# Column halves for layer 1's attention products, and a moved multiply by C in layer 1's state-space mixer

## The chip, the core and the metric

The kernel runs on one core of one Trainium2 chip, as one launch. Its metric is the device time of that launch in microseconds. A core has a matrix engine (TensorE, PE in the views; its weight loads are PEld), a vector engine (VectorE, DVE), an engine for activation functions and copies (ScalarE, ACT), a general one (GpSimd, POOL) and a queue that issues transfers (SyncE, SP). TensorE multiplies a stationary operand ("weights", at most 128 rows by 128 columns) with streamed columns and writes to PSUM[...]. A product that needs fewer rows or columns can use a part of the array, a tile of it, and several tiles work at once.

## What is computed

A perceiver of four layers: a latent x of 2 x 256 tokens with 256 features attends to a context of 2 x 4096 tokens, then passes self-attention or a mixer, and a feed-forward part, in each layer. All of it is float32. Two parts of layer 1 matter here. The first is its cross-attention with 16 heads of 64 (written out from the kernel's names and the weights' shapes in the reference):

```python
B, S, D = (4, 512, 256)
H, DK, DV = (16, 64, 64)
'Wq': jax.random.normal(ks[3], (H, D, DK), jnp.float32) * sd, 'bq': ...
'Wo': jax.random.normal(ks[9], (H * DV, D), jnp.float32) * sd, 'bo': ...
```

For each head, queries come from the normalised latent, keys and values from the context, and x + softmax(q k^T) v Wo + bo goes on. The second is the state-space mixer:

```python
delta = jax.nn.softplus(dtr @ W_dt + 2.0 * dt_bias).reshape(b, l, G, D_STATE)
A = -jnp.exp(A_log).reshape(G, D_STATE, D_STATE)
a = jnp.exp(delta[..., None] * A)
bb = (delta * x)[..., None] * Bg[:, :, :, None, :]
...
_, h = lax.associative_scan(comb, (a, bb), axis=1)
y = jnp.einsum('blgpn,blgn->blgp', h, Cg).reshape(b, l, D_INNER)
y = (y + D * xf) * jax.nn.silu(z)
return y @ W_out
```

so h[t] = a[t] h[t-1] + bb[t] along the tokens, weighed by C and summed over the 16 states.

## The kernel before

The layers run one after the other. Every float32 product is two passes of TensorE, so one `matmul` of the code is two weight loads and two matmuls in the trace. In both parts below the order of the instructions on TensorE, VectorE, ScalarE and GpSimd is the order of the code (`in_order`, L338, ties each instruction to the one before on its engine).

**Layer-1 cross-attention (`l1_xattn`, L973).** A unit u is one pair of heads of one batch element: 8 pairs times 2 elements, 16 units. Each passes over the context in 8 blocks of 512 tokens; g counts all 128 blocks. A trip of the loop (L1158) does, on TensorE: `weigh` of block g-10 (L1090; probabilities times values, the two heads in the two halves of the array's columns, so its weights are 64 columns wide, 128 x 64); in some trips the products below; `keys` of block g+1 (L1019; 128 x 128 weights, 512 streamed columns, two of them, through the helper `mm`, L355); `values` of block g-9 (L1026; 128 x 128 weights, 128 streamed columns, 4 x 2 of them); `scores` of block g (L1037; the two heads in the two halves of the array's rows, 64 x 128 weights). Once in a unit come: `sums` at the end of the unit's last `weigh` (L1104; a product with ones, 64 columns wide), `out` at g % 8 = 2 (L1141), `query` at g % 8 = 5 (L1013), and at g % 8 = 0 `turned` (L1116, four transposes of the running maxima, between keys and values) and `repeat` (L1127, four more, between values and scores).

The other engines follow: ScalarE copies the scores to SBUF (L1058), VectorE keeps their maxima (L1061), later subtracts the unit's maximum (L1072), ScalarE takes the exponential (L1075), GpSimd adds up the totals (L1086). VectorE copies the values (L335), ScalarE the keys (L1024). `combine` (L1111) and `maxima` (L1122) are VectorE's, on either side of `turned`. PSUM has four banks "mm" (scores, query, sums, turned, out), two "tr" (keys, values), one "dec" (the repeated maxima) and one accumulator for `weigh`.

**Layer-1 mixer (`l1_attn`, L1224).** 64 columns of states are taken in 32 pairs. For pair k: `b_columns` (L1329) repeats B on TensorE and copies it on ScalarE; `drives` (L1336) makes the decay on ScalarE into a bank "dec" (L1343) and multiplies B by delta x on GpSimd (L1345); one step of the softplus of later columns goes to ScalarE and GpSimd (L1218, L1219) in each trip; `states` (L1351) repeats C on TensorE (L1326) into a bank "mm", and on VectorE scans the two batch elements one after the other (L1357) and multiplies by C (L1360); `add_up` (L1363) adds the states on TensorE (L1368). A trip issues states(k), b_columns(k+2), drives(k+1), add_up(k-1). There are three banks "mm", two "tr", two "dec".

Of the kernel before, what the change touches and what calls it, by code (L numbers as in the profile page):

```python
# [22 lines left out]
P = 128  # L23
B = 2
L = 256
# [4 lines left out]
KC = D // P  # L30
# [238 lines left out]
class Perceiver:  # L269
# [85 lines left out]
    def mm(self, out, pairs):  # L355

        for i, (lhsT, rhs) in enumerate(pairs):
            self.nc.tensor.matmul(out, lhsT, rhs, start=i == 0, stop=i == len(pairs) - 1)  # L358
# [614 lines left out]
    def l1_xattn(self, x, cpool):  # L973
# [9 lines left out]
        nc = self.nc  # L983
        with ExitStack() as s:
# [3 lines left out]
            xnT = self.to_T(self.layernorm(x))  # L988
            wq, wk, wv, wo = (self.weight(f"l1x_w{n}") for n in "qkvo")
# [8 lines left out]
            halves = [slice(0, 64), slice(64, 128)]  # L998
            order = [(hh, i) for i in range(2) for hh in range(2)]
            ctx, q, kT, v, score = {}, {}, {}, {}, {}  # L1000
            most, low, spread, total, av, sums, rec, z = {}, {}, {}, {}, {}, {}, {}, {}
# [7 lines left out]
            def for_values(g):  # L1009

                return ("k", g + 8) if g + 8 < G and (g + 8) // 64 == g // 64 else ("v", g)

            def query(u):  # L1013
                ps = self.bank([P, L])
                self.mm(ps, [(wq[:, k, ts(u % 8, P)], xnT[:, k, ts(u // 8, L)]) for k in range(KC)])
                q[u] = p2.tile([P, L], F32, name="qT", tag="qT")
                return lambda: nc.vector.tensor_scalar_add(q[u], ps, self.col("l1x_bq", u % 8))

            def keys(g):  # L1019
                pr = g // 8 % 8  # L1020
                ps = self.bank([P, 512], "tr")
                self.mm(ps, [(wk[:, k, ts(pr, P)], ctx["k", g][:, k, :]) for k in range(KC)])
                kT[g] = p2.tile([P, 512], F32, name="kT", tag="kT")
                nc.scalar.activation(kT[g], ps, AF.Identity, bias=self.col("l1x_bk", pr))  # L1024

            def values(g):  # L1026
                pr = g // 8 % 8
                ps = self.bank([P, 4, P], "tr")
                for i in range(4):
                    self.mm(  # L1030
                        ps[:, i, :],
                        [(ctx[for_values(g)][:, k, ts(i, P)], wv[:, k, ts(pr, P)]) for k in range(KC)],
                    )
                v[g] = p2.tile([P, 4, P], F32, name="v", tag="v", bufs=3)
                self.copy(g < G - 8, v[g], ps)
# [80 lines left out]
            def turned(u):  # L1116
                ps = self.bank([P, 4, P])
                for i in range(4):
                    nc.tensor.transpose(ps[:, i, :], low[u][:, i // 2, ts(i % 2, P)], self.ident)
                low[u] = ps  # L1120

            def maxima(u):  # L1122
# [18 lines left out]
            def out(u):  # L1141
                ps = self.bank([P, 2, D])
                for qt in range(2):
                    self.mm(ps[:, qt, :], [(z[u][:, ts(qt, P)], wo[:, u % 8, :])])
                two = y[:, ts(u // 8, 2), :]
                return lambda: nc.vector.tensor_add(two, ps, two)

# [9 lines left out]
            with self.in_order(e.PE, e.DVE, e.Activation, e.Pool):  # L1157
                for g in range(-1, G + 12):  # L1158
# [7 lines left out]
                    u = g // 8 - 1 if g % 8 == 0 and 0 < g <= G else None  # L1166
# [6 lines left out]
                    if g % 8 == 2 and made(g - 11):  # L1173
                        evacs.append(out((g - 11) // 8))
                    if (g == -1 or g % 8 == 5) and made(g + 3):
                        evacs.append(query((g + 3) // 8))
# [5 lines left out]
                    if made(g + 1):  # L1182
                        keys(g + 1)
                    if u is not None:
                        turned(u)
# [6 lines left out]
                    if made(g - 9) and g <= G:  # L1192
                        values(g - 9)
                    if made(g - 8) and g >= G:
                        values(g - 8)
# [28 lines left out]
    def l1_attn(self, x):  # L1224
# [3 lines left out]
        nc = self.nc  # L1228
        T = NT * P
        with ExitStack() as s:  # L1230
# [17 lines left out]
            xnT = self.to_T(self.layernorm(x))  # L1248
# [19 lines left out]
            low, high = pool.tile([P, 4, T], F32, name="low"), pool.tile([P, 4, T], F32, name="high")  # L1268
# [50 lines left out]
            pairs = [(j, q, rs) for j in range(4) for q in range(4) for rs in ((0, 1), (2, 3))]  # L1319
            spread, decay, drive, weighed, sums = {}, {}, {}, {}, {}  # L1320

            def columns(mat, rows_of, j, q, rs, tag):
                got = [self.bank([P, T], tag) for _ in rs]
                for r, ps in zip(rs, got):
                    rows = ts(r, 32)
                    nc.tensor.matmul(ps, mat[rows, ts(q, P)], rows_of[rows, j, :], start=True, stop=True)  # L1326
                return got
# [23 lines left out]
            def states(k):  # L1351
                got = columns(mats["c"], cT, *pairs[k], "mm")
                weighed[k] = []
                for a, bb, c in zip(decay.pop(k), drive.pop(k), got):
                    h = p4.tile([P, T], F32, name="state", tag="state")
                    for b in range(B):
                        nc.vector.tensor_tensor_scan(  # L1357
                            h[:, ts(b, L)], a[:, ts(b, L)], bb[:, ts(b, L)], 0.0, ALU.mult, ALU.add
                        )
                    nc.vector.tensor_mul(h, c, h)  # L1360
                    weighed[k].append(h)

            def add_up(k):  # L1363
                j, q, rs = pairs[k]
# [13 lines left out]
            with self.in_order(e.PE, e.DVE, e.Activation, e.Pool):  # L1378
                n = len(pairs)
                for k in range(-2, n + 1):  # L1380
                    if 0 <= k < n:
                        states(k)
                    if k + 2 < n:
                        b_columns(k + 2)
                    if 0 <= k + 1 < n:
                        drives(k + 1)
                    step = next(made, None)
                    if step is not None:
                        step()
                    if k > 0:  # L1390
                        add_up(k - 1)
                self.conv_hidden("tr", "tr", "dec")
                return self.linear(yz, wout, x)
# [1196 lines left out]
```

## Time and profile before

Three runs took 2627.75, 2615.05 and 2627.32 us, median 2627.32. The execution that was profiled took 2616.86 us, of which the span from the first instruction to the last is 2615.1.

| | whole span | attention, 310 to 1240 us |
|---|---|---|
| length, us | 2615.1 | 930.0 |
| TensorE busy, us | 2480.0 (95%) | 928.83 |
| its weight loads, us | 1659.1 (63%) | 643.38 |
| VectorE busy, us | 1713.5 (66%) | 695.14 |
| ScalarE busy, us | 1343.4 (51%) | 582.28 |
| GpSimd busy, us | 919.3 (35%) | 546.43 |
| granted TensorE clock | 0.96 | 1.00 |

The largest groups of matmuls in the attention, by line, operands, weights' shape, streamed columns and count, with busy time and mean length of one:

```profile
L1051 PE MATMUL ps_mm<-qT,kT 64*128 64x256 f32 x2048 | 255.7, 389 | 0.0
L1098 PE MATMUL acc<-S,v 128*64 128x256 f32 x2048 | 250.1, 385 | 0.5 <-DVE rec L1136 0.4
L358 PE MATMUL ps_tr<-ctxT,w_l1x_wk 128*128 128x512 f32 x512 | 250.6, 612 | 0.0
L358 PE MATMUL ps_tr<-w_l1x_wv,ctxT 128*128 128x128 f32 x2048 | 249.9, 275 | 0.0
```

A row of such a view names the line, the engine, what is written from what, and the shape: "128*64" is rows by columns of the weights, "128x256" the streamed operand. A matmul's length includes its way through the array, so lengths overlap; the distance between starts is what a matmul costs. The keys and values carry the helper's line, L358.

### The profile page before, as it was taken

To read this page: it belongs to the slowest core of one execution; us is meant where nothing else is said; L and a number is where in the kernel's file an instruction comes from. 1 tells how busy PE (TensorE), PEld (TensorE's weight loads), DVE (VectorE), ACT (ScalarE), POOL (GpSimd) and SP (SyncE) were. 2 spreads that over 40 slices of the span, in tenths; PEclk is the share of its full clock that TensorE was granted. 3 is DMA by queue.
4 is the path that set the end of the run, shared out by engine and by line. 5 is a ranking of instruction groups with operands and counts; after the bars stand their busy time and mean duration, and the time that the engine had idled before them with its cause. 6 is when DMAs were issued, how large, how long until landed. Compare 5 with 4: busy or idle time off the path is not lost.

```text
span 2615.1 us, 45590 instructions
## 1 busy us (share of the span) xinstructions
PE 2480.0 (95%) x17701; PEld 1659.1 (63%) x17701; DVE 1713.5 (66%) x3184; ACT 1343.4 (51%) x2540; POOL 919.3 (35%) x864
## 2 busy tenths in 40 slices
PE   8987999999999999999799998899989999999889
PEld 6854566666666666666533565556935666664678
DVE  5566577777777777777769755544267888854642
ACT  3323666666666666666466421432215777784512
POOL 0520255555555555556639413001101222210010
PEclk9988999999999999999899998789999999999889
DMA  6210322222232222222210100005730000003656
GB/s 256 89 57 30 118 65 65 67 72 65 65 113 82 70 69 65 65 67 81 80 65 1 65 20 22 4 25 214 266 147 18 2 2 2 2 2 123 218 213 223
DMA packets 77255, 214.24 MB, mean 82 GB/s; under 512 B 6408, under 2 KB 21456, under 8 KB 66544
## 3 DMA queue, kind: packets, MB, share of 16 engines
q1 hardware_dynamic: 72128, 202.69, 23.4%
q0 software_dynamic: 1888, 5.90, 0.7%
q8 instruction: 139, 2.28, 0.4%
q10 hardware_dynamic: 3024, 2.75, 0.3%
q14 instruction: 76, 0.62, 0.1%
HBM read 190.48 MB, written 20.84 MB: 81 GB/s over the span
## 4 chain that ended last, share of the span: by engine, by line
PE 39%; DVE 6%; issue 2%; ACT 2%; POOL 2%; DMA 0%; another core or an unknown queue 0%; DVEq 0%; ACTq 0%; POOLq 0%; SPq 0%
PE ps_mm L358 10%; PE ps_mm L2172 5%; PE ps_tr L2216 5%; PE ps_tr L2200 4%; PE ps_tr L358 3%; PE acc L358 3%; PE ps_mm L785 2%; DVE state L1357 1%; POOL spread L1345 1%; PE ps_tr L2335 1%; PE acc L826 1%; PE ps_tr L801 1%; PE ps_tr L2378 1%; PE ps_mm L2360 1%; PE acc L1583 1%
## 5 line engine op out<-in xcount | busy, mean ns | idle before, releaser
L1086 POOL TENSOR_TENSOR total<-total,S 128x512 f32<-128x512 f32 x434 | 540.8, 1278 | 299.6 <-ACT S L1075 299.2
L1075 ACT ACTIVATE S<-S 128x512 f32<-128x512 f32 x512 | 302.3, 625 | 209.0 <-DVE S L1072 208.8
L2176 DVE TENSOR_REDUCE mx<-ps_mm 128x1 f32<-128x512 f32 x512 | 317.9, 684 | 73.0 <-PE ps_tr L2200 54.2
L1061 DVE TENSOR_TENSOR most<-ps_mm,most 128x512 f32<-128x512 f32 x448 | 278.3, 684 | 119.2 <-ACT S L1058 119.2
L1058 ACT COPY S<-ps_mm 128x512 f32<-128x512 f32 x512 | 262.8, 600 | 115.3 <-PE ps_mm L1051 114.5
L1072 DVE TENSOR_TENSOR S<-S,ps_dec 128x512 f32<-128x512 f32 x512 | 317.6, 680 | 1.3 <-PE ps_dec L1130 1.3
L2204 ACT ACTIVATE PT<-ps_tr 128x512 f32<-128x512 f32 x476 | 246.7, 603 | 74.6 <-PE ps_tr L2200 71.8
L358 PEld LDWEIGHTS ps_tr<-w_l1x_wv,ctxT 128*128 128x128 f32 x2048 | 246.9, 192 | 52.5 <-issue 52.2
L1051 PE MATMUL ps_mm<-qT,kT 64*128 64x256 f32 x2048 | 255.7, 389 | 0.0
L1098 PE MATMUL acc<-S,v 128*64 128x256 f32 x2048 | 250.1, 385 | 0.5 <-DVE rec L1136 0.4
L358 PE MATMUL ps_tr<-ctxT,w_l1x_wk 128*128 128x512 f32 x512 | 250.6, 612 | 0.0
L2172 PE MATMUL ps_mm<-kT,qT 32*128 32x512 f32 x1024 | 250.1, 618 | 0.2 <-DVE mx L2176 0.2
L358 PE MATMUL ps_tr<-w_l1x_wv,ctxT 128*128 128x128 f32 x2048 | 249.9, 275 | 0.0
L2200 PE MATMUL ps_tr<-qm,kT 32*128 32x256 f32 x1904 | 238.3, 388 | 0.0
L1051 PEld LDWEIGHTS ps_mm<-qT,kT 64*128 64x128 f32 x2048 | 187.3, 186 | 38.3 <-DVE most L1061 3.8
L1098 PEld LDWEIGHTS acc<-S,v 128*64 128x64 f32 x2048 | 136.1, 136 | 97.3 <-ACT S L1058 38.8
L2200 PEld LDWEIGHTS ps_tr<-qm,kT 32*128 32x128 f32 x1904 | 171.0, 184 | 15.6 <-issue 6.2
L2225 POOL TENSOR_TENSOR sums<-sums,part 128x256 f32<-128x256 f32 x102 | 73.7, 722 | 257.1 <-ACT part L2224 257.1
L358 PEld LDWEIGHTS ps_tr<-ctxT,w_l1x_wk 128*128 128x128 f32 x512 | 89.2, 189 | 100.6 <-issue 99.1
L335 DVE COPY v<-ps_tr 128x512 f32<-128x512 f32 x120 | 82.9, 690 | 89.0 <-PE ps_tr L358 88.9
L2216 PE MATMUL ps_tr<-PT,v 128*32 128x256 f32 x2048 | 139.6, 385 | 0.3 <-ACT PT L2204 0.3
L2172 PEld LDWEIGHTS ps_mm<-kT,qT 32*128 32x128 f32 x1024 | 86.3, 185 | 61.3 <-issue 49.9
(542 smaller groups left out, 3808.8 us busy)
## 6 DMA issues: line engine op xcount, KB each, us to landing
ctxT<-in_ctxT SPq DMA_DIRECT2D x144, 512.0 KB, 3.6
ctxT<-in_ctxT SPq DMA_DIRECT2D x16, 1024.0 KB, 5.7
w_l2f_gu<-in_l2f_gu SPq DMA_DIRECT2D x16, 1024.0 KB, 7.1
bd_dram<-bd SPq DMA_DIRECT2D x8, 1536.0 KB, 5.5
w_l3f_w<-in_l3f_w SPq DMA_DIRECT2D x11, 1028.0 KB, 9.8
w_l3f_w<-in_l3f_w SPq DMA_DIRECT2D x11, 1024.0 KB, 5.1
ctx<-in_ctx SPq DMA_DIRECT2D x8, 1024.0 KB, 4.9
w_l2f_down<-in_l2f_down SPq DMA_DIRECT2D x16, 512.0 KB, 5.3
```

The source lines that it names most:

```text
L358: self.nc.tensor.matmul(out, lhsT, rhs, start=i == 0, stop=i == len(pairs) - 1)
L1051: nc.tensor.matmul(banks[hh, i][:, j, :], k[part, ts(2 * i + j, P)], q[u][part, :], start=True, stop=True)
L1058: nc.scalar.copy(t, ps)
L1061: nc.vector.tensor_tensor(m, ps, m, ALU.max)
L1072: nc.vector.tensor_tensor(t, t, spread[u][:, hh, :].unsqueeze(1).to_broadcast([P, 2, L]), ALU.add)
L1075: nc.scalar.activation(t, t, AF.Exp)
L1086: nc.gpsimd.tensor_add(tot, tot, t)
L1098: nc.tensor.matmul(av[u][part], vs[:, 2 * i + j, part], got[hh, i][:, j, :], start=g % 8 == 0 and i + j == 0, stop=g % 8 == 7 and i + j == 2,)
L2172: nc.tensor.matmul(ps, qT[rows, 2 * half + c, ts(t, P)], kT[rows, ts(j, 512)], start=True, stop=True,)
L2176: nc.vector.tensor_reduce(mx[:, c, r, j : j + 1], ps, AX.X, ALU.max)
L2200: nc.tensor.matmul(ps[:, i, :], kT[rows, ts(2 * u + i, P)], q[rows], start=True, stop=True)
L2216: nc.tensor.matmul(ps[ts(r, 32), :], v[:, 2 * u + i, :], pt[:, i, :], start=i == 0, stop=i == 1)
```

## The change

In the attention a local `mm` replaces the helper for query, keys, values and out, and the transposes of `turned` become products with the identity through it too. It issues every product twice, for weight columns 0 to 63 and 64 to 127, the second half into the other 64 partitions of the same bank. `scores`, `weigh`, the sums and `repeat` stay as they were. In the mixer the multiply by C of a pair's first column is issued after the first scan of its second column; before, it came ahead of it. Nothing is moved past a transfer, and the order on ScalarE, GpSimd and SyncE is the same.

```diff
+            def mm(ps, pairs):
+
+                for k, (a, b) in enumerate(pairs):
+                    for part in halves:
+                        nc.tensor.matmul(ps[part], a[:, part], b, start=k == 0, stop=k == len(pairs) - 1)
+
             def query(u):
                 ps = self.bank([P, L])
-                self.mm(ps, [(wq[:, k, ts(u % 8, P)], xnT[:, k, ts(u // 8, L)]) for k in range(KC)])
+                mm(ps, [(wq[:, k, ts(u % 8, P)], xnT[:, k, ts(u // 8, L)]) for k in range(KC)])
...
-                self.mm(ps, [(wk[:, k, ts(pr, P)], ctx["k", g][:, k, :]) for k in range(KC)])
+                mm(ps, [(wk[:, k, ts(pr, P)], ctx["k", g][:, k, :]) for k in range(KC)])
...
                 for i in range(4):
-                    self.mm(
+                    mm(
                         ps[:, i, :],
                         [(ctx[for_values(g)][:, k, ts(i, P)], wv[:, k, ts(pr, P)]) for k in range(KC)],
                     )
...
                 for i in range(4):
-                    nc.tensor.transpose(ps[:, i, :], low[u][:, i // 2, ts(i % 2, P)], self.ident)
+                    mm(ps[:, i, :], [(low[u][:, i // 2, ts(i % 2, P)], self.ident)])
...
                 for qt in range(2):
-                    self.mm(ps[:, qt, :], [(z[u][:, ts(qt, P)], wo[:, u % 8, :])])
+                    mm(ps[:, qt, :], [(z[u][:, ts(qt, P)], wo[:, u % 8, :])])
...
-                for a, bb, c in zip(decay.pop(k), drive.pop(k), got):
+
+                for i, (a, bb) in enumerate(zip(decay.pop(k), drive.pop(k))):
                     h = p4.tile([P, T], F32, name="state", tag="state")
+                    weighed[k].append(h)
                     for b in range(B):
                         nc.vector.tensor_tensor_scan(
                             h[:, ts(b, L)], a[:, ts(b, L)], bb[:, ts(b, L)], 0.0, ALU.mult, ALU.add
                         )
-                    nc.vector.tensor_mul(h, c, h)
-                    weighed[k].append(h)
+                        if (i, b) == (1, 0):
+                            nc.vector.tensor_mul(weighed[k][0], got[0], weighed[k][0])
+                nc.vector.tensor_mul(h, got[1], h)
```

## The prediction

> **What bounds the kernel now.** I read the busy table by stretches first, then TensorE's timeline within the layer-1 attention, then VectorE's, TensorE's and GpSimd's timelines within the mixer. Columns of the first view: stretch, then for each engine busy us (instructions), granted clock, DMA share, GB/s.
>
> ```profile
> 400.00:500.00 100.00, 99.83 (x699) 69.52 (x698) 73.62 (x118) 62.42 (x115) 57.88 (x47) 1.00 0.22 65
> 600.00:700.00 100.00, 99.83 (x697) 69.62 (x698) 73.82 (x118) 62.37 (x115) 58.78 (x48) 1.00 0.23 66
> ...
> 1362.00:1382.00 20.00, 20.00 (x64) 7.28 (x63) 18.96 (x32) 14.82 (x27) 16.48 (x14) 1.00 0.00 2
> ```
>
> In attention TensorE alone is full at full clock; VectorE (74%), ScalarE (62%), GpSimd (58%) and the DMA have room. In the mixer TensorE is full too and VectorE at 95%.
>
> Busy does not mean streaming, so I took the starts (start us, length, engine, line, operation, count):
>
> ```profile
> 746.93 1.95 PE L1098 MATMUL acc<-S,v 128*64 128x256 f32 x16
> 748.71 1.08 PE L358 MATMUL ps_mm<-total,ones 128*64 128x256 f32 x8
> 749.72 1.98 PE L358 MATMUL ps_tr<-ctxT,w_l1x_wk 128*128 128x512 f32 x4
> ...
> 763.71 1.95 PE L1098 MATMUL acc<-S,v 128*64 128x256 f32 x16
> 765.59 1.98 PE L358 MATMUL ps_tr<-ctxT,w_l1x_wk 128*128 128x512 f32 x4
> 767.41 1.95 PE L358 MATMUL ps_tr<-w_l1x_wv,ctxT 128*128 128x128 f32 x16
> 769.29 2.00 PE L1051 MATMUL ps_mm<-qT,kT 64*128 64x256 f32 x16
> ...
> 780.60 1.13 PE L358 MATMUL ps_mm<-xT,w_l1x_wq 128*128 128x256 f32 x4
> 781.56 1.88 PE L358 MATMUL ps_tr<-ctxT,w_l1x_wk 128*128 128x512 f32 x4
> 783.28 1.95 PE L358 MATMUL ps_tr<-w_l1x_wv,ctxT 128*128 128x128 f32 x16
> ```
>
> Start to start, weigh (L1098, 64 weight columns) takes 748.71-746.93 = 1.78 us when 64-column work follows, but 765.59-763.71 = 1.88 us when full-width keys follow. Keys take 767.41-765.59 = 1.82 us right after weigh, but 783.28-781.56 = 1.72 us after the full-width query. So the step from 64-column to full-width tiles costs 0.10 + 0.10 = 0.20 us (93 + 104 = 197 ns by the trace's starts): TensorE empties, then the first load is not hidden. One context block is weigh 1.88 + keys 1.82 + values 1.88 + scores 1.93 = 7.51 us.
>
> Does a half-width product keep pace at 128 streamed columns, as values would? Layer 3 has it:
>
> ```profile
> 2438.75 1.08 PE L2390 MATMUL acc<-PT,values 128*32 128x128 f32 x32
> 2439.76 0.59 PE L2335 MATMUL ps_tr<-rT,qv 32*128 32x384 f32 x2
> ```
>
> 32 matmuls in four column tiles, 8 rounds, 1.01 us to the next tile shape; less 0.09 to empty and 0.05 for the first load, 0.109 us a round.
>
> In the mixer VectorE runs scan, scan, multiply by C (L1360), and again:
>
> ```profile
> 1452.73 1.26 DVE L1357 TENSOR_TENSOR_SCAN state<-ps_dec,spread 128x256 f32<-128x256 f32 x2
> 1454.10 0.69 DVE L1360 TENSOR_TENSOR state<-ps_mm,state 128x512 f32<-128x512 f32 x1
> 1454.71 1.26 DVE L1357 TENSOR_TENSOR_SCAN state<-ps_dec,spread 128x256 f32<-128x256 f32 x2
> ```
>
> A column takes 1454.71-1452.73 = 1.975 us, a pair 3.95. The starts are 0.60 (scan), 0.77 (scan to multiply), 0.61 (multiply to scan): the multiply waits 0.17 us for the scan it reads. TensorE's own pair, where it never stops, is
>
> ```profile
> 1365.90 1.98 PE L1368 MATMUL acc<-state,ident 128*128 128x512 f32 x4
> 1367.81 1.13 PE L1326 MATMUL ps_mm<-cT,mat_c 32*128 32x512 f32 x4
> 1368.78 1.02 PE L1326 MATMUL ps_tr<-bT,mat_b 32*128 32x512 f32 x4
> 1369.73 1.98 PE L1368 MATMUL acc<-state,ident 128*128 128x512 f32 x4
> ```
>
> 3.83 us, and GpSimd's two spread products plus one delta product 2.50 + 1.27 = 3.77 us.
>
> **What the Trainium skill says.** "TensorEngine Tiling (Array Packing)", Key Properties: "Changing tiling mode (not just tile) drains the TensorE"; tiles load and multiply in parallel. The trace agrees: 0.197 us at weigh to keys, nothing at weigh to sums. Same page, Restrictions: column tiling excludes transpose mode for FP32; that is why `turned` becomes a plain matmul. "TensorE: Matmul & The Clock Gate", LDWEIGHTS: load time goes with weight columns; here loads read 137 ns at 64 columns, 190 at 128. "VectorE: DVE Perf Modes", The DRAIN you can't avoid: a same-engine read after write needs a semaphore or one intervening VectorE op; the 0.77 against 0.60 us above is that semaphore.
>
> **The change, part by part.** Sums are against the profiled execution: 2616.86 us, span 2615.1.
>
> *Weigh to keys.* Weigh, sums, out, query, keys, turned and values now all have 64-column tiles, so the change of shape after weigh goes: 0.197 us. Values to scores and scores to weigh keep theirs. Weigh meets keys in blocks g = 10 to 127, 118 times; 14 of them (g = 16, 24, ... 120) hold the turned maxima and are counted apart. 104 x 0.197 = 20.5 us.
>
> *Pace of keys and values.* Twice the matmuls at half the width, two at a time: keys stay at 0.429 us a round (weigh's pairs keep full pace: 0.216 us per 256 columns, 0.429/2). Values now need (1.88-0.09)/16 = 0.1115 us a round; I take the 0.109 of L2390: 16 x 0.0023 = 0.037 us, 104 times, 3.8 us. Bounds: 0 if the 0.1115 stays; a loss if rounds get longer (rival C).
>
> *Blocks with the turned maxima.* In the same timeline four transposes took 742.39-741.95 = 0.44 us; as fp32 matmuls each makes two passes, 8 rounds x 0.109 = 0.87: +0.44. After values the repeat (L1130, full width) now meets a change of shape. From weigh: 1.73 + 1.72 + 0.87 + 1.75 + 0.09 = 6.16 us to the repeat. Before, it began at 744.42, weigh at 738.25, 6.17 us earlier, because it waited for VectorE's reduction of the maxima, which ends when VectorE's queue allows. Thus 0, bounds -0.2 to +0.1 us each, -3 to +1.4 in all.
>
> *Start and end of attention.* Blocks 0 to 7 alternate keys and scores; the load after scores is 64 columns, 8 x 0.05 = +0.4 us, paid back by the first turned (+0.44), on which all engines wait. In the last blocks (g > 127) values and weigh alternate without any change of shape, 0.34 us for each of 6 blocks, but TensorE already waits 3.62 us for GpSimd's totals there: no gain. The last turned sits on the path: -0.5 us.
>
> What hides the rest: VectorE needs 0.74 x 7.51 = 5.6 us of a block of 7.27. The copied values land 1.1 us before weigh, the exponentials 1.6 us, the banks of scores 3 us: no wait takes over 0.23 us. Context loads are at 24% of the DMA. Sum: 20.5 + 3.8 + 0 - 0.5 = 23.8 us. What follows starts with the mixer's weight load (win, 6.84 us), which is issued when attention's buffers are freed, so it moves along.
>
> *Mixer.* New order: scan, scan, scan, multiply first column, scan, multiply second. The first multiply's input is finished during the third scan, so one of two 0.17 us waits goes: VectorE's pair 3.95 - 0.17 = 3.78 us. Then TensorE's 3.83 is late next, and GpSimd's 3.77 is close: 0.12 us for each of the some 26 pairs from 1362 us on: 3.1 us. Before 1362 TensorE is the bound (projections between): 0. The moved multiply passes only the third scan, which needs the second column's decay and spread; ScalarE can make that decay once the scans of the previous pair's second column are through, over 1 us ahead. It frees its C bank 0.43 us later; the bank is wanted some 2 us later. Bounds: 0 (GpSimd's chain with delta keeps 3.95) to 5 us (0.17 x 27 and the hiccups at each eighth pair shrink). I take 3.
>
> Sum: 23.8 + 3 = 26.8 us.
>
> **From sum to forecast.** The executions of before lie at two levels, 2615.05 and 2616.86, and 2627.32 and 2627.75; the profile doesn't say why. 26.8 off the profiled 2616.9 is 2590; off the median 2627.3 it is 2600.5. I forecast 2597, between, nearer the median.
>
> **Rivals.**
> *B: half of it.* A bank or semaphore wait hides behind the 0.09 us in which TensorE empties and stays, or the turned blocks lose their 0.2 us, or the mixer gives nothing. For: out and query take banks of scores, whose release the emptying would mask. Against: weigh to sums runs on without a gap. 10 to 14 us gained: 2613 to 2617 from the median.
> *C: slower.* The two halves of one product stream the same columns, and 4 instructions are due every 0.109 us; if halves run one after the other, or instructions come too late, values pay. It decides from 0.109 + 0.234/16 = 0.124 us a round; at 0.15 us 118 x (16 x 0.041 - 0.197) = 54 us are lost: 2680; fully serial, values and keys cost 1.7 us each a block, over 400 us. For: weigh's halves stream different data. Against: L2390 does 8 instructions in 0.109 us over a run of 64, as long as the 64 of values; the rest of a block is sparser.
> *D: the mixer turns against itself,* as the first accumulate or ACT waits: 2 to 3 us back, 2602; it stays within the forecast's range.
>
> **Chances.** Forecast, with D, 0.78 (its own range 2586 to 2606: 21 to 31 us off either level); B 0.16; C 0.06. About 0.5%, 13 us, is what a measurement of this kernel can tell from no change. B falls half on each side of it: faster 0.78 + 0.08 = 0.86, same 0.08, slower 0.06. The range reaches into B: 2584 to 2614.
>
> **What would show it.** Weigh to keys 1.73 us start to start and keys 1.72 in every block; a block 7.27 us; values 16 rounds in 1.84 to the scores; turned 0.87; TensorE's matmuls up by 2880 (512 keys, 2048 values, 64 query, 64 out, 192 turned); the mixer's pair 3.83 us with TensorE without gaps, VectorE's first multiply 0.60 us after the third scan. The prediction is wrong if rounds of values exceed 0.124 us, if keys still start 0.3 us after weigh's last matmul, or if the mixer's pair stays at 3.95.

## The result and the profile after

The changed kernel took 2594.41, 2588.19, 2587.97 and 2593.47 us, median 2590.83; the kernel before, beside it, 2627.75, 2615.05, 2627.32 and 2617.16, median 2622.24. The ratio is 0.9884, with a 95% interval of 0.986 to 0.9908: a gain of 24 to 37 us. The profiled execution took 2594.41 us with a span of 2592.6.

The busy table by stretches of the changed kernel (stretch, length; for PE, PEld, DVE, ACT and POOL busy us and instructions; granted clock, DMA share, GB/s):

```profile
400.00:500.00 100.00, 100.00 (x1000) 68.72 (x998) 77.39 (x123) 64.08 (x118) 57.96 (x48) 1.00 0.23 70
600.00:700.00 100.00, 100.00 (x986) 68.58 (x986) 76.80 (x122) 62.97 (x117) 58.29 (x47) 1.00 0.24 70
1362.00:1382.00 20.00, 20.00 (x66) 7.17 (x68) 19.22 (x32) 13.33 (x24) 19.90 (x17) 1.00 0.00 0
```

TensorE still is the full engine. That its share only rose from 99.83 to 100.00 while the stage became 24 us shorter shows how little this figure can tell. VectorE, with the same work in less time, went from 74 to 77%. The groups of matmuls in the attention (310 to 1215 us) show the new shapes:

```profile
L1017 PE MATMUL ps_tr<-w_l1x_wv,ctxT 128*64 128x128 f32 x3744 | 225.0, 273 | 0.0
L1017 PE MATMUL ps_tr<-ctxT,w_l1x_wk 128*64 128x512 f32 x936 | 221.4, 592 | 0.0
```

Keys and values are now "128*64" and carry the line of the local `mm`, L1017; a matmul of values is as long as before (273 against 275 ns), though there are twice as many of them. Now the order on TensorE (start us, length, engine, line, operation, count), first four blocks without extras, then one with the turned maxima:

```profile
753.26 1.89 PE L1017 MATMUL ps_tr<-ctxT,w_l1x_wk 128*64 128x512 f32 x8
754.98 1.92 PE L1017 MATMUL ps_tr<-w_l1x_wv,ctxT 128*64 128x128 f32 x32
756.82 2.00 PE L1057 MATMUL ps_mm<-qT,kT 64*128 64x256 f32 x16
758.75 1.95 PE L1104 MATMUL acc<-S,v 128*64 128x256 f32 x16
760.53 1.89 PE L1017 MATMUL ps_tr<-ctxT,w_l1x_wk 128*64 128x512 f32 x8
...
788.69 1.95 PE L1104 MATMUL acc<-S,v 128*64 128x256 f32 x16
790.47 1.89 PE L1017 MATMUL ps_tr<-ctxT,w_l1x_wk 128*64 128x512 f32 x8
792.18 1.04 PE L1017 MATMUL ps_mm<-ident,low 128*64 128x128 f32 x16
793.05 1.92 PE L1017 MATMUL ps_tr<-w_l1x_wv,ctxT 128*64 128x128 f32 x32
794.90 0.65 PE L1136 MATMUL ps_dec<-ident,nm 128*128 128x128 f32 x4
```

Read the distances of the starts: keys 754.98-753.26 = 1.72 us, values 1.84, scores 1.93, weigh 760.53-758.75 = 1.78. A block is 7.27 us where it was 7.50. The starts of `weigh`, one line for the eight blocks of a unit (the one with 8.7 holds the turned maxima; 8.1 to 8.4 hold out, query or sums), show that the gain is the same in every other block:

```
before  8.37 7.50 7.50 8.37 7.50 7.50 8.68 8.42
after   8.13 7.27 7.27 8.13 7.27 7.27 8.72 8.18
```

In the mixer, VectorE of the changed kernel:

```profile
1428.21 1.84 DVE L1365 TENSOR_TENSOR_SCAN state<-ps_dec,spread 128x256 f32<-128x256 f32 x3
1429.97 0.66 DVE L1369 TENSOR_TENSOR state<-ps_mm,state 128x512 f32<-128x512 f32 x1
1430.55 0.68 DVE L1365 TENSOR_TENSOR_SCAN state<-ps_dec,spread 128x256 f32<-128x256 f32 x1
1431.33 0.69 DVE L1370 TENSOR_TENSOR state<-ps_mm,state 128x512 f32<-128x512 f32 x1
1431.94 1.84 DVE L1365 TENSOR_TENSOR_SCAN state<-ps_dec,spread 128x256 f32<-128x256 f32 x3
```

VectorE's pair is 1431.94-1428.21 = 3.73 us (3.95 before): three scans 1.76, the first multiply 0.58 without a wait, the fourth scan 0.78 to the multiply that reads it, and 0.61. TensorE takes 3.83 without a gap (its sums of two neighbouring pairs start at 1428.90 and 1432.73). The distances between the starts of the sums of neighbouring pairs, from the third sum to the last, tell where the mixer's time went:

```
before  3.83 x11, 3.88 3.95 4.67 3.88 3.95 3.94 3.95 3.95 3.95 3.95 4.67 3.89 3.95 3.95 3.95 3.09 3.95 2.90
after   3.83 x15, 3.87, 3.83 x10, 2.97 3.30 2.68
```

For 11 distances the two kernels are alike; only then had VectorE of before fallen behind far enough for TensorE to wait for it. The trace of before shows this lead shrink by about 0.12 us a pair: the first multiply of a pair ends 3.73 us ahead of the sum at 1369.73, 2.02 us ahead of the one at 1404.2, and 1.96 us ahead of the one at 1408.1, where the distances start to grow.

Now the whole, cut at the starts of named instructions. "Blocks" is from the first `weigh` to the last `scores`, "tail" from there to the last `out`, "start" from the mixer's first product to its first sum, "pairs" from there to the first product of layer 2, "rest" from there to the end, and the last column is how long TensorE's clock stood at half in the rest (a stretch at half clock that the end of the kernel cuts off isn't counted).

| kernel | span | blocks | tail | start | pairs | rest | half clock in the rest |
|---|---|---|---|---|---|---|---|
| before | 2615.1 | 936.76 | 53.37 | 43.87 | 126.53 | 1137.45 | 150.18 |
| after | 2592.6 | 912.96 | 54.64 | 45.61 | 122.00 | 1140.82 | 160.43 |

Blocks -23.8, tail +1.3, pairs -4.5: 27.0 us in the stretches that the change touches. The spans differ by 22.5 only, because start and rest, in which both kernels issue the same products, were 5 us longer in this execution.

### The profile page after: what moved, and what is told of

Its sections match the earlier page's. It is cut to its first block, busy times and chain, and to the rows that moved or that the text cites. A ratio compares the mean times of both kernels' runs of the same rounds, so it can differ in the third digit from the quotient of the medians.

```text
span 2592.6 us, 51423 instructions
## 1 busy us (share of the span) xinstructions
PE 2457.8 (95%) x20579; PEld 1637.4 (63%) x20581; DVE 1709.5 (66%) x3184; ACT 1342.6 (52%) x2540; POOL 921.2 (36%) x864
## 4 chain that ended last, share of the span: by engine, by line
PE 41%; DVE 5%; issue 2%; ACT 2%; POOL 1%; DMA 0%; DVEq 0%; ACTq 0%; POOLq 0%; SPq 0%
PE ps_mm L358 10%; PE ps_mm L2181 5%; PE ps_tr L2225 5%; PE ps_tr L2209 4%; PE ps_tr L358 3%; PE acc L358 3%; PE ps_mm L785 2%; PE ps_tr L2344 1%; DVE state L1365 1%; PE acc L826 1%; PE ps_tr L2387 1%; POOL spread L1351 1%; PE ps_tr L801 1%; PE acc L1377 1%; PE acc L1592 1%
## 5 line engine op out<-in xcount | busy, mean ns | idle before, releaser
L1017 PEld LDWEIGHTS ps_tr<-w_l1x_wv,ctxT 128*64 128x64 f32 x4096 | 235.4, 137 | 58.4 <-issue 57.7
L1017 PE MATMUL ps_tr<-w_l1x_wv,ctxT 128*64 128x128 f32 x4096 | 248.2, 273 | 0.0
L1017 PE MATMUL ps_tr<-ctxT,w_l1x_wk 128*64 128x512 f32 x1024 | 242.4, 593 | 0.4 <-PE ps_mm L1017 0.4
L1017 PEld LDWEIGHTS ps_tr<-ctxT,w_l1x_wk 128*64 128x64 f32 x1024 | 75.8, 137 | 91.3 <-issue 74.7
```

Of the source, the lines that this page charges most:

```text
L1017: nc.tensor.matmul(ps[part], a[:, part], b, start=k == 0, stop=k == len(pairs) - 1)
```

## The experiments

Two questions were open: whether the attention's gain comes from the removed change of tile shape or from the half width itself (each product cheaper), and whether the mixer gives anything. Diffs are against the changed kernel.

| run | median us (of one run where no ratio stands) | ratio to before, interval | blocks | tail | start | pairs | rest | half clock |
|---|---|---|---|---|---|---|---|---|
| attn_only | 2598.63 | 0.9917 [0.9903, 0.9931] | 912.96 | 56.07 | 43.75 | 126.55 | 1135.11 | 143.36 |
| mixer_only | 2613.80 | 0.9967 [0.9955, 0.9979] | 936.78 | 53.94 | 46.21 | 122.05 | 1139.42 | 150.19 |
| mixer_third | 2609.97 | 0.9979 [0.9959, 0.9999] | 936.73 | 53.80 | 46.69 | 122.03 | 1128.08 | 136.53 |
| values_full | 2616.78 | 0.9977 [0.9966, 0.9987] | 938.67 | 53.81 | 43.87 | 122.01 | 1130.88 | 143.36 |
| turned_transposed | 2587.82 | 0.9867 [0.9850, 0.9884] | 912.31 | 54.74 | 46.75 | 121.99 | 1137.50 | 150.18 |
| halves_in_series | 2596.12 | 0.9890 [0.9871, 0.9909] | 918.34 | 55.00 | 46.84 | 122.00 | 1135.67 | 146.77 |
| no_wait_multiplies | 2593.35 | 0.9884 [0.9866, 0.9902] | 912.97 | 54.67 | 45.67 | 122.60 | 1137.64 | 153.60 |
| last_totals_on_pe | 2586.78 | 0.9863 [0.9843, 0.9882] | 912.97 | 50.16 | 43.72 | 122.32 | 1138.36 | 153.60 |
| sums_in_twos | 2605.17 | 0.9942 [0.9925, 0.9959] | 912.97 | 54.67 | 52.70 | 130.91 | 1137.52 | 150.19 |
| both_more | 2599.36 | 0.9922 [0.9901, 0.9943] | 912.96 | 50.16 | 53.17 | 127.57 | 1146.26 | 177.49 |
| before_again | 2617.54 | | 936.73 | 53.71 | 46.42 | 126.47 | 1134.99 | 143.36 |
| mixer_again | 2609.22 | | 936.72 | 53.27 | 43.63 | 121.98 | 1136.09 | 143.36 |

A stretch repeats within 0.1 us in "blocks", and within 0.4 in "pairs", where it isn't edited; "start" swings by 3 us and "rest" by 18 where nothing in them was changed. In `attn_only` the tail is 56.07 us, because the clock stood at half for a further 3.41 us in it, from 1226.80 us on. So the stretches carry the findings below, and the times check them.

**The two parts alone.** Attention alone:

```diff
-                for i, (a, bb) in enumerate(zip(decay.pop(k), drive.pop(k))):
+                for a, bb, c in zip(decay.pop(k), drive.pop(k), got):
...
-                        if (i, b) == (1, 0):
-                            nc.vector.tensor_mul(weighed[k][0], got[0], weighed[k][0])
-                nc.vector.tensor_mul(h, got[1], h)
+                    nc.vector.tensor_mul(h, c, h)
+                    weighed[k].append(h)
```

> Only the attention's column halves; the mixer as before. If the halves carry the gain: from the first weigh to the last scores 913 us as in the changed kernel (936.8 before), VectorE's pair in the mixer back at 3.95 us, from the mixer's first sum to its end 126.5 us; time 0.990 to 0.991 of before, some 25 us less. If the mixer carries more than its 3 us, or helps the attention, this one stays at 0.995 or above.

The mixer alone is the other half: the kernel before with the new `states`.

> Only the moved multiply; the attention as before. If one of two 0.17 us waits goes and TensorE is late next: from the mixer's first sum to its end 122 us (126.5 before), pairs at 3.83 us with TensorE without gaps, time 0.998 to 0.999 of before, which is below what this kernel's time can tell. If the 4.5 us seen in that stretch were chance of the clock or of the start, it stays at 126 us.

The blocks gain all their 23.8 us with attention alone and nothing with the mixer alone; the pairs the other way round, 4.5. The parts don't touch each other. In time, attention alone gave 21.8 us (2623.47 x 0.0083; interval 18 to 25), the mixer alone 8.7 (6 to 12), more than its pairs show. A further run of each kernel, on one chip, and a third timing of the mixer alone were to tell chance from a hidden gain.

> The kernel before, unchanged, for a second profile. Its first profiled execution was at the lower end of its times (2616.9 us against a median of some 2623). If what is left over between the sums by stage and the times is the clock that TensorE is granted: the stages that run at full clock repeat to 0.1 us (936.8 us from the first weigh to the last scores, 126.5 from the mixer's first sum to its end), and the stages with a half clock differ by several us, in step with the time at half clock. If a stage of the attention or mixer itself runs in two ways, it shows here.

> The kernel with only the moved multiply, for a second profile: its time was 8.7 us below before, and the stretch from the mixer's first sum to its end only 4.5. If the rest is the granted clock: 122.0 us again in that stretch, and the rest of the span moves with the time at half clock. If the moved multiply helps elsewhere in the mixer: the stretch from the mixer's first projection to its first sum is below 43.8 us in both profiles (it was 46.2 in the first).

> The moved multiply alone, timed once more. The trace of this edit shows 4.5 us gained between the mixer's first sum and its end, and its first timing said 8.7 us. If the trace names all of the gain: 4 to 6 us below the kernel before, a ratio of 0.9977 to 0.9985. If something outside that stretch also gains: 8 to 9 us again, 0.9965 to 0.997.

The pairs repeated: 126.47 before, 121.98 and 122.03 with the moved multiply. The two single runs took 2617.54 (before; a second run of it beside them took 2626.12) and 2609.22. The third timing gave 0.9979, 5.5 us with an interval of 0.3 to 11. All agree with 4.5 but the first, whose interval just misses it; no stretch outside the pairs is shorter in all the traces. What remains of the 8.7 is best read as scatter of the rest; it isn't proven.

**Width or shape?** Only values go back to full width, so that the change of shape moves from after `weigh` to before values:

```diff
                 for i in range(4):
-                    mm(
+                    self.mm(
```

> As the changed kernel, but values keep full-width weights; keys, query, turned and out stay in halves. If the change of tile shape is the price: it moves from weigh and keys to keys and values, a block is 7.268 + 0.197 + 0.037 = 7.50 us, from the first weigh to the last scores 937 us as before, time that of before less the mixer's 3 to 4. If narrower weights are faster by themselves (shorter loads), keys keep a part: 925 us or less.

TensorE of this run:

```profile
764.87 1.95 PE L1104 MATMUL acc<-S,v 128*64 128x256 f32 x16
766.64 1.89 PE L1017 MATMUL ps_tr<-ctxT,w_l1x_wk 128*64 128x512 f32 x8
768.46 2.05 PE L358 MATMUL ps_tr<-w_l1x_wv,ctxT 128*128 128x128 f32 x16
770.44 2.00 PE L1057 MATMUL ps_mm<-qT,kT 64*128 64x256 f32 x16
```

Weigh is 1.77 and keys follow without a loss, as in the changed kernel. But keys now take 768.46-766.64 = 1.82 (1.72 where half-width values follow), and values 770.44-768.46 = 1.98 (1.84 there). The block is back at 7.50 us, and the stretch at 938.67; the 1.9 us above before lie in the blocks with the turned maxima, 8.81 us against 8.68. So half width by itself earns nothing: keys at half width take 1.72 us without a change of shape beside them, as the full-width keys behind query did, and the price lies in the change of shape, wherever it stands. 0.10 us is paid before it, as TensorE empties; of the 0.14 behind it, 0.04 is the pace of values that the prediction had worked out.

**The turned maxima as transposes again.**

```diff
-                    mm(ps[:, i, :], [(low[u][:, i // 2, ts(i % 2, P)], self.ident)])
+                    nc.tensor.transpose(ps[:, i, :], low[u][:, i // 2, ts(i % 2, P)], self.ident)
```

> As the changed kernel, but the maxima are turned by four full-width transposes as before. Saved: 4 rounds of 0.109 = 0.44 us a unit for the second pass; paid: two changes of shape, keys to transposes and transposes to values, 0.39 us. If both prices hold: 912 to 914 us from the first weigh to the last scores (913.0 changed), same time. If only the passes count, 6 to 7 us less; if a transpose pays more than a matmul for the change of shape, more than 915 us.

```profile
789.17 1.89 PE L1017 MATMUL ps_tr<-ctxT,w_l1x_wk 128*64 128x512 f32 x8
790.99 0.66 PE L1125 MATMUL ps_mm<-ident,low 128*128 128x128 f32 x4
791.57 1.97 PE L1017 MATMUL ps_tr<-w_l1x_wv,ctxT 128*64 128x128 f32 x32
793.56 0.65 PE L1136 MATMUL ps_dec<-ident,nm 128*128 128x128 f32 x4
```

The transposes bring two changes of shape back: keys 1.82, transposes 0.58, values 1.99, against 1.71, 0.87 and 1.85 in the changed kernel. That is 4.39 against 4.43 us: 0.24 us more for keys and values, 0.29 less for the transposes, which make one pass; the two prices almost cancel. (Here the repeat starts 0.06 us behind the end of VectorE's reduction, as before the change, and 0.10 to 0.11 in the changed kernel; so a little of the 1.99 can be a wait for VectorE.) The blocks are 0.65 us shorter in all (912.31), which the time (0.9867) can't tell from the changed kernel's. Its block of the turned maxima is 8.68 again, as before.

**Does the neighbour matter?** The two halves of a product that share the streamed columns are issued one after the other in the changed kernel, pass by pass. Here the first half makes all its products before the second begins:

```diff
-                for k, (a, b) in enumerate(pairs):
-                    for part in halves:
+                for part in halves:
+                    for k, (a, b) in enumerate(pairs):
```

> As the changed kernel, but each product issues its first column half for all its terms and then its second half, so that two neighbours in TensorE's order are of the same half. If TensorE looks ahead and pairs the halves by itself, as the sums in the trace suggest (first head's terms, then the second's, 8 matmuls in 0.86 us): 913 to 917 us from the first weigh to the last scores. If only neighbours run side by side, keys lose up to 1.3 us a block and values more: 1000 us or above, and the pairing is what the local helper is for.

```profile
757.26 1.94 PE L1017 MATMUL ps_tr<-ctxT,w_l1x_wk 128*64 128x512 f32 x8
758.98 1.97 PE L1017 MATMUL ps_tr<-w_l1x_wv,ctxT 128*64 128x128 f32 x32
760.88 2.00 PE L1057 MATMUL ps_mm<-qT,kT 64*128 64x256 f32 x16
```

The block is 7.32 us: keys keep their 1.72 and values take 1.90 instead of 1.84, where serial halves would have cost, by the prediction's estimate, 1.7 us more for each of the two. Matmuls that aren't neighbours in the order still ran side by side in the two halves of the array. The order in the code costs 5.4 us over the stretch (918.34), not hundreds; rival C was further away than the prediction thought.

**VectorE or TensorE in the mixer?** A pair's second multiply also goes behind the next scan, so that no multiply waits:

```diff
+                        if (i, b) == (0, 0):
+                            run(second)
...
-                nc.vector.tensor_mul(h, got[1], h)
+                second.append(partial(nc.vector.tensor_mul, h, got[1], h))
```

> As the changed kernel, but the multiply of a pair's second column is issued after the next pair's first scan too, so that no multiply waits for the scan before it. VectorE's pair would be 3.5 to 3.6 us. If TensorE's 3.83 us is the bound after the change: from the mixer's first sum to its end 122 us, as in the changed kernel. If VectorE still sets it, 117 us or less.

VectorE of this run, from one pair's last two scans to the next pair's, with the delayed multiply (L1361) behind them:

```profile
1428.65 1.26 DVE L1371 TENSOR_TENSOR_SCAN state<-ps_dec,spread 128x256 f32<-128x256 f32 x2
1429.83 0.66 DVE L1361 TENSOR_TENSOR state<-ps_mm,state 128x512 f32<-128x512 f32 x1
...
1432.17 1.26 DVE L1371 TENSOR_TENSOR_SCAN state<-ps_dec,spread 128x256 f32<-128x256 f32 x2
```

Here VectorE does a pair in 1432.17-1428.65 = 3.52 us, and it gains nothing: the pairs take 122.60, with two distances between sums of 4.15 and 4.52 us and most others at 3.83. Through most of this run VectorE's pair takes 3.7 to 3.9 us, because its scans then wait for GpSimd's products. GpSimd is the nearest rival for the bound: in the changed kernel it is busy 19.90 of the 20 us shown above, and its own pair takes 3.69 us (1384.02-1380.33). But behind its last delta product (1417.20) it comes to idle 1.33 us a pair (from 1436.05 us on), and the sums stay 3.83 us apart. So TensorE's 3.83 is the bound since the change, as the prediction had it, with GpSimd close behind.

**The end of attention.** There the changed kernel lost. TensorE at the last sums and at `out`, first of before, then of the changed kernel, with the idle time ahead and what ended it in brackets:

```profile
1292.39 1.09 PE L358 MATMUL ps_mm<-total,ones 128*64 128x256 f32 x8 [3.62 <-POOL total L1086]
1298.01 2.08 PE L358 MATMUL ps_mm<-w_l1x_wo,zT 128*128 128x256 f32 x4 [2.85 <-ACT zT L1139]
```

```profile
1268.64 1.98 PE L358 MATMUL ps_mm<-total,ones 128*64 128x256 f32 x8 [5.87 <-POOL total L1092]
1270.42 1.57 PE L358 MATMUL ps_mm<-rest,ones 128*64 128x256 f32 x4
1274.83 1.93 PE L1017 MATMUL ps_mm<-w_l1x_wo,zT 128*64 128x256 f32 x8 [2.85 <-ACT zT L1145]
```

TensorE finishes its last `weigh` earlier and waits 5.87 us (3.62 before) for GpSimd's totals. So the totals of the last block were given to TensorE, as four more products with ones for each head; GpSimd's and VectorE's additions for it fall away:

```diff
+                    if g == G - 1:
+                        continue
...
                         terms = [total[u][:, hh, j, :] for j in range(2)]
+                        if g == G - 1:
+                            terms = [got[hh, i][:, j, :] for i in range(2) for j in range(2)] + terms
```

> As the changed kernel, but the probabilities of the very last context block are summed by TensorE (four more terms for each head in the last product with ones) and not added by GpSimd and VectorE. If GpSimd's totals set the end of the attention, so that TensorE's faster last blocks are worth nothing: from the last scores to the last out 50.5 us (54.6 changed), time some 4 us below the changed kernel. If TensorE's own work or VectorE's late sums set it: 54 to 56 us.

```profile
1262.81 1.67 PE L358 MATMUL ps_mm<-S,ones 128*64 128x256 f32 x7
1264.82 0.43 PE L358 MATMUL ps_mm<-total,ones 128*64 128x256 f32 x1 [0.33 <-POOL total L1094]
...
1271.35 1.08 PE L1017 MATMUL ps_mm<-w_l1x_wo,zT 128*64 128x256 f32 x8 [2.85 <-ACT zT L1149]
```

The wait is 0.33 us, and the tail 50.16 instead of 54.64. Part of this is the clock. The busy table of the sums and of `out` (stretch, length, PE busy, granted clock, DMA share, GB/s), two rows of before, then two of the changed kernel:

```profile
1292.40:1295.20 2.80, 2.76 (x12) 0.68 0.00 0
1298.00:1300.20 2.20, 2.08 (x4) 0.50 0.00 0
1268.60:1272.00 3.40, 3.34 (x12) 0.57 0.00 0
1274.80:1277.00 2.20, 1.93 (x8) 0.53 0.00 0
```

and with the totals on TensorE:

```profile
1262.60:1268.60 6.00, 5.57 (x32) 1.00 0.00 0
1271.30:1272.50 1.20, 1.08 (x8) 1.00 0.00 0
```

Behind the wait, be it 3.62 or 5.87 us, TensorE runs at 0.50 to 0.68 of its clock and takes 2.08 and 1.93 us for `out`; without the wait it runs at full clock (1.08). The 12 traces that have the wait show a mean clock of 0.50 to 0.72 in the sums, the two without it 1.00. This is the fastest of all versions, median 2586.78 (2585.56 to 2590.60). Its gain over the changed kernel, 4.5 us, is seen in the trace; the two ratios' intervals overlap.

**TensorE's load in the mixer.** If TensorE is the bound, each pair's sum may be the place to save: the sums are issued for two pairs at once, which halves the changes between its shapes; `state` gets 8 buffers for it.

```diff
-                    h = p4.tile([P, T], F32, name="state", tag="state")
+                    h = p4.tile([P, T], F32, name="state", tag="state", bufs=8)
...
-                    if k > 0:
+                    if k > 0 and k % 2 == 0:
+                        add_up(k - 2)
                         add_up(k - 1)
```

> As the changed kernel, but the mixer adds up two pairs in every second trip (with eight buffers for states, not six), so that TensorE changes its tile shape twice in two pairs, not four times. If TensorE's 3.83 us a pair is the bound and a change of shape costs it some 0.19 us: TensorE's pair would need 3.64 us, VectorE's 3.73 sets the pace, and from the mixer's first sum to its end (less the one trip that the first sum starts later) some 2.5 us go; time 2 to 3 us below the changed kernel, which only the trace can tell. If another wait comes in its place (the state buffers, GpSimd's 3.7 us with ScalarE's delta), the pairs stay at 3.83 us or above.

> The changed kernel with both: the last block's totals on TensorE and the mixer's sums in twos. If the two are independent: from the last scores to the last out 50.2 us, the mixer's pairs as in the run with sums in twos, time some 7 us below the changed kernel, 0.985 to 0.986 of before.

A miss. The pairs are 130.91 us, 9 more than in the changed kernel, and the first sum comes 7 us later. One part of this is a wait. From the table of waits of this run, 1350 to 1480 us (engine, line, what it waited for: us, times, longest):

```profile
ACT spread L1340 <- PE ps_tr L1332: 37.3, 16, 5.8
...
PE ps_mm L1332 <- DVE state L1369: 4.8, 8, 1.3
```

In the changed kernel (1335 to 1458) the first of these is shorter and the second is not there:

```profile
ACT spread L1340 <- PE ps_tr L1332: 24.4, 25, 3.0
```

In trips without sums TensorE comes to the next pair's C right after B, and waits for a bank of C that VectorE's multiply still holds; B stands behind it, so ScalarE waits too. Two pairs took 7.82 us at best, 3.91 each, against 3.83.

The larger part is the clock. The pairs in the busy table (columns as above), with the sums in twos, with both edits, and in the changed kernel:

```profile
1337.11:1468.02 130.91, 125.44 (x353) 0.92 0.00 1
1333.96:1461.53 127.57, 122.09 (x354) 0.95 0.00 1
1329.79:1451.79 122.00, 121.04 (x370) 1.00 0.00 1
```

TensorE's clock stood at half for 20.48 us of the pairs in the first, for 13.65 us in the second, and not at all in the pairs of any other run. ScalarE's longest wait, 5.8 us up to 1378.33, falls into such a stretch (1368.33 to 1375.16). The two runs have the same mixer and the same wait for C (4.8 us), yet `both_more` took 3.34 us less: it had 6.83 us less at half clock, and half of that is 3.4. The kernel with both edits thus kept the tail's gain (50.16) and most of the mixer's loss (127.57).

From the mixer's first product to its end, start and pairs together, the sums in twos took 183.61 us against 167.61. Counted at full clock (an estimate: each time less half of its time at half clock, 32.71 and 11.22 us), 5.3 of these 16.0 us are left, about the size of the waits. Whether the waits brought the clock down, and whether sums in twos would pay without them, was not tested.

## Why the prediction was right, and where not

**Weigh to keys, 20.5 us: right.** Weigh takes 1.78 and keys 1.72 in every block, and `values_full` shows the price to be one of shape, not of width. **Values, 3.8 us: right.** The rounds keep 0.109-0.110 us (first to last start of 16 rounds 1.644 us, over 15), though both halves stream the same columns. Together predicted 24.3, measured 23.8 in the blocks.

**Blocks with the turned maxima, 0: nearly.** They lost 0.04 us each, some 0.6 us in all, within the bounds. From weigh to repeat the prediction added up 6.16 us; it is 794.90-788.69 = 6.21, mostly because weigh took 1.78 us there and not the 1.73 that the sum put in; the prediction's own line had 1.78 for weigh ahead of 64-column work. With that TensorE overtook the wait for VectorE as what is late; with transposes it is 793.56-787.39 = 6.17 again.

**End of attention, -0.5: undersized.** The tail lost 1.3 us. The totals came 0.85 us later after the last scores (1268.64-1221.49 = 47.15 us, before 1292.39-1246.09 = 46.30). Of this 0.42 is the turned products (0.89 us against 0.47), the part foreseen. Another 0.24 lies ahead of them and was not in the sum: ScalarE, busy with exponentials, starts to copy the last scores 0.10 us after the last of them starts, before the change 0.14 us ahead of it, and the maxima follow this copy. The other 0.43 came behind the wait, from the sums' start to the last `out` (7.49 against 7.06 us). The prediction looked at the wait as free time for TensorE and didn't ask what clock it leaves; but it left a low clock in before too, where the same stretch took 6.96 to 7.59 us in five traces. So the 0.43 can't be put down to the longer wait.

**Mixer, 3.1 us: right in mechanism, wrong in its terms.** The first multiply starts 0.58 us after the third scan and TensorE holds 3.83 us. But "0.12 us for each of the some 26 pairs" was not what happened: the distances above show 13 plain pairs that lost 1.35 us together, because VectorE first had to use up the lead it had. The two hiccups of 4.67 us at eighth pairs, which the prediction left to its upper bound, gave 1.68, the last three distances 0.99, and the end behind the last sum 0.6 (less 0.04 at the one distance of 3.87): 4.5 us, to rounding. The 3.77 us for GpSimd was a sum of lengths, which overlap; by starts its pair takes 3.69, so it left a little more room than the prediction gave it. Rival D is refuted: the mixer alone gained.

**Sum: 26.8 predicted, 27.0 in the traces.** Blocks 23.8, tail -1.3, pairs 4.5; that they agree to 0.2 us is luck in part, since the blocks (0.5 short) and the tail (0.8) lost about what the mixer gave on top (1.5).

**From sum to forecast: the weak step.** "The executions of before lie at two levels" was read from three runs. 19 runs of before on one chip lie from 2614.74 to 2627.26 with no gap of more than 2.2 us but the one above the lowest (2614.74 to 2619.08). The profiled run was near the low end. The measured median is 6.2 us under the forecast: from the measured median of before, 2622.24, the same sum would have given 2595.4, within the measured interval of the ratio. That the forecast of 2597 is 0.9885 of the median it started from, and 0.9884 was measured, is luck: the sum names 26.8 us, the medians lie 31.4 apart, and the traces account for 27.0 of that.

**Rivals.** B (half of it) falls, since no block hides the 0.09 us of emptying: keys follow weigh 1.78 us after its start, and keys and values take the 1.72 and 1.84 us that were forecast. C falls by the rounds of 0.110 us, and by `halves_in_series` even when the order invites it.

## What to carry over

Count the changes of tile shape on TensorE, by start-to-start distances and not by its busy share: here each cost about 0.2 us, and neighbours that agree in shape were worth 24 us even at twice the matmuls. When a wait on VectorE goes, it is worth only the distance to the next engine's pace, and only from the pair on at which its lead is used up. Where an engine gets faster ahead of a wait for another, look at that wait and the clock behind it: a few products moved onto the idle TensorE took back more than the change had lost there. And before a longer stretch is put down to a wait, look at the clock that it ran at.

## What the runs showed of the hardware

**Halves find each other.** Two 64-column matmuls ran at once not only as neighbours but with the other half's products up to four matmuls away in the order (keys in `halves_in_series`: 1.72 us for 8 matmuls of 512 columns, as when interleaved); values lost 0.05 us a block.

**The scatter goes with the clock.** In 14 traces the rest, with the same instructions in each, took 1128 to 1146 us. It goes with the time that TensorE's clock stood at half (correlation 0.92, 0.40 us per us). Longest and shortest in the busy table (both_more, then mixer_third; columns as above):

```profile
1461.54:2607.80 1146.26, 1071.77 (x8972) 0.92 0.25 89
```

```profile
1475.35:2603.40 1128.05, 1054.37 (x8972) 0.94 0.25 91
```

TensorE's busy time alone differs by 17.40 of the 18.19 us: the products take longer, not the waits between them. "Start" shows the same: where its products weren't edited it took between 43.63 us (`mixer_again`, 6.15 us at half clock) and 46.84 (`halves_in_series`, 12.86), 0.48 us per us.

The Trainium skill, "TensorE: Matmul & The Clock Gate", Part 1, What's actually happening, says that the clock is at half by default and after an idle window, and that these windows, 3413 ns long, run free of the kernel. The traces agree on the length: the times at half clock in the table, 136.53 to 177.49 us, are whole multiples (40, 42, 43, 44, 45, 47, 52) of 3.413 us. On "idle" they don't: with the sums in twos the clock fell at 1368.33 us, though TensorE had been busy for 2.14 of the 3.41 us before, its only wait being one of 1.27 us. What decides it isn't shown here. It seems likely, but was not tested, that an edit that moves the work by a few us against these windows can shift the time by several us anywhere behind it; a gain below that is read from its own stretch.
